# A short-convolution attention and a 16-expert layer on one core: the experts' narrow feature block first, and another order for the first tile

## The chip, the cores and the metric

The kernel runs on one core of a Trainium2 chip. The metric is the device time of one execution in microseconds (us). Names used below: TensorE (PE in the profile, with its weight loads as PEld), VectorE (DVE), ScalarE (ACT), GpSimd (POOL), and SP, the queue that issues most DMAs. Each engine works through its own instructions in program order and waits for others through semaphores; the order in the program is therefore the schedule.

## The reference, cut to what matters

All data is float32. `x` and the context are 8 batches of 256 rows of 512 features: 2048 rows (`T`), in 16 tiles of 128.

```python
# attention: k = v = context, q = layernorm(x), heads of 8 rows, 32 heads
kv  = einsum('bhil,bhjl->bijhl', k, v)          # products of rows of one head
out = causal_convolution(kv, ssm_kernel) + kv * D
out = einsum('bijhl,bhil->bjhl', out, q)
x   = x + out
# experts: 16 experts, the best 4 for each row, 256 slots each, inner width 352
h      = layernorm(x)
scores = softmax(h @ gate_w.T); topk_w, topk_i = top_k(scores, 4)    # weights normalised
xg     = tokens gathered for each expert                              # 16 x 256 x 512
mid    = silu(xg @ w_gate) * (xg @ w_up)                              # 512 -> 352
y      = scatter_add((mid @ w_down) * weight)                         # 352 -> 512
x      = x + y + (silu(h @ sw_gate) * (h @ sw_up)) @ sw_down          # shared part, width 704
```

## The kernel before

The schedule is written by hand: every engine gets its instructions in the order in which the program calls them.

**Attention.** A loop over 16 tiles of 128 rows, two heads each, in the order 1, 0, 2, 3, ... (tile 1 is `FIRST`, because its convolution matrices come straight from the input). `heads_of` transposes a tile on TensorE and copies it out of PSUM twice on ScalarE (L418, L419); `normalise` writes the normalised rows on ScalarE (L369 `nmr`, L370); `products` multiplies rows of k, one instruction for each of four chunks on GpSimd (L443, L445, and L451 for later heads). `attend` runs the convolutions as matmuls (L468) into one of two PSUM tiles `y`, and VectorE multiplies by q and sums (L501 to L518); the last sums are on GpSimd or VectorE (L520, L521). The PSUM pool `ps_tr` has two buffers under one tag for all transposes, logits and warm-up transposes (`stir`, L669). Ahead of the loop, tile 1's k is transposed, then its x is normalised, eight warm-up transposes run, and q is transposed. `begin` finishes a convolution matrix, `pads` and `windows` write the others to memory, from where they are loaded (`toep`); the shared weights (`swg`, `swu`, `swt`, `swd`) follow on SP, nine pieces for a tile.

**What fills TensorE.** `fill(n)` runs n steps of the shared part (L154, L168, L185) between the attention's steps. Every fourth tile `logits_of` computes the router's logits of four tiles (L592) and copies them to `exch` on ScalarE (L600); `turn_logits` transposes that (L612) and copies it to `logits` on VectorE (L615), and `choose` picks the experts of one tile at a time.

**Experts.** A loop over 16 experts. The weights of expert e + 2 are loaded at the end of iteration e into two buffers (`w`, `wd`). An expert's 352 inner features are blocks of 128, 128 and 96: `NI` is 3, `NW` is 2, the last block (index 2) is the narrow one. `gate_up` takes a wide block with 16 float32 matmuls (L1025; each is two instructions), a silu on ScalarE (L1032) and a product on VectorE (L1033). The narrow block uses weights packed side by side by `pack` on ScalarE into the one buffer `wt` (L1008): 8 matmuls of 64 columns for gate and up of the last 32 features (L1037) and 4 of 128 columns for the first 64 (L1045), then silu and product in three pieces (L1054, L1055, L1058, L1059). `down` multiplies the three blocks for each half of the 256 slots (L1067), scales (L1075) and adds the rows to `out` by an indirect DMA on GpSimd's queue (L1076); every such scatter waits for the one before to land. Between gate-up and down stand, for the experts ahead, `tokens` (L994, L404 on VectorE), `find` (L911 on TensorE, L919 to L934 on VectorE) and `gather` (L968, GpSimd). `find` and `gather` serve expert e + 3 and so end with expert 12; `shuffle` (`slots`, `gb`, on SP) follows the weights' load.

The last expert does its two halves one after the other, so that the first half's scatter runs under the second half's matmuls.

Of the kernel before, what the change touches and what calls it, by code (L numbers as in the profile page):

```python
# [20 lines left out]
P = 128  # L21
# [7 lines left out]
HT = R // HD  # L29
HB = HD * B  # L30
E, K, CAP, I, IS = 16, 4, 256, 352, 704
# [22 lines left out]
def ssm_attention__then__moe_kernel(  # L54
# [22 lines left out]
    nc = tc.nc  # L77
# [182 lines left out]
    with ExitStack() as att:  # L260
# [11 lines left out]
        FIRST = 1  # L272
# [140 lines left out]
        def heads_of(src, width, name):  # L413


            dst = half.tile([P, NC, HT, width], F32, name=name)
            pt = transpose_in(src).rearrange("p c (h w) -> p c h w", h=HT)
            nc.scalar.copy(dst[:, :, :, 0:HB], pt)  # L418
            nc.scalar.copy(dst[:, :, :, HB:width], pt[:, :, :, 0 : width - HB])  # L419
            return dst  # L420
# [14 lines left out]
            )  # L435
            return toep if head < PLAIN else toep.rearrange("p m q -> p (m q)")

        def products(head, hh, k2):

            kv = work.tile([P, NC + 1, PAIRS], F32, name="kv", bufs=3)  # L440
            kh = k2[:, :, hh, :]
            kc = kh.ap[1][0]
            nc.gpsimd.tensor_mul(kv[:, 0:NC, ND * HB :], kh[:, :, 0 : HB // 2], kh[:, :, HB // 2 : HB])  # L443
            for c in range(NC):
                nc.gpsimd.tensor_mul(  # L445
                    kv[:, c, 0 : ND * HB].rearrange("p (d w) -> p d w", d=ND),
                    kh[:, c, 0:HB].unsqueeze(1).broadcast_to([P, ND, HB]),
                    view(kh[:, c, :], 0, [[B, ND], [1, HB]]),
                )
            if head >= PLAIN:  # L450
                nc.gpsimd.tensor_add(kv[:, NC, :], kv[:, 0, :], kv[:, 1, :])  # L451
            return kv
# [229 lines left out]

        qn = load.tile([P, L], F32, name="qn", tag="kn")
        stats = first_statistics(xs[:, FIRST, :])
        k2 = heads_of(loaded.pop(FIRST), KW, "k2")
        normalise(qn, xs[:, FIRST, :], *stats)
        begin(0)
        kvs = [products(FIRST * HT, 0, k2)]
        stir(8)
        q2 = heads_of(qn, QW, "q2")  # L690
        toeps.update({FIRST * HT + hh: firsts[hh] for hh in range(HT)})
        stats = first_statistics(xs[:, 0, :])
# [31 lines left out]
        for n in range(NT):  # L724
            more = n + 1 < NT
            swift = n + 1 in SWIFT
            t = seq[n]
            oT = work.tile([P, NC, P], F32, name="oT")
            tps = [toeps.pop(t * HT + hh) for hh in range(HT)]
            if swift and more:  # L730
                got_k = fetch_blocks(sent_k)
            if more and n:
                for hh in range(HT):
                    load_blocks(seq[n + 1] * HT + hh)
            if swift and more:
                got_q = fetch_blocks(sent_q)
            for i in range(2 if n == 0 else n + 3, min(n + 4, NT)):
                loaded[i] = load_tile(i)
            load_shared(9)
            attend(t * HT + 0, 0, 0, tps[0], kvs[0], q2, oT)  # L740
            if n == 0:
                begin(1)
                kvs.append(products(t * HT + 1, 1, k2))
            if n - 2 in MILD:
                transpose_blocks(xnT[:, :, n - 2, :], got_x)
            choose()
            if more and not swift and n:
                qn = load.tile([P, L], F32, name="qn", tag="kn")
                stats = statistics(qn, xs[:, seq[n + 1], :])
            fill(2)  # L750
            if n + 2 in SWIFT:
                kp, kp_by_block = in_blocks("kp")
                kp_stats = statistics(kp_by_block, chunked(xs[:, n + 2, :]))

            attend(t * HT + 0, 0, 2, tps[0], kvs[0], q2, oT)
            if more and not swift:
                if n == 0:
                    qn = load.tile([P, L], F32, name="qn", tag="kn")
                k_next = heads_of(loaded.pop(seq[n + 1]), KW, "k2")
                normalise(qn, xs[:, seq[n + 1], :], *stats)  # L760
            if n > 0:
                total = add_to_x(seq[n - 1], oT_done)
            fill(2)
            if n > 0:
                xn, xstats = new_statistics(seq[n - 1], total)
            if more:
                if swift:
                    k_next = heads_from(got_k, KW, "k2")
                kv_next = [products(seq[n + 1] * HT, 0, k_next)]

            attend(t * HT + 1, 1, 0, tps[1], kvs[1], q2, oT)
            if more and not swift:
                q_next = heads_of(qn, QW, "q2")
            if n == 0:
                pg = ps_tr.tile([P, NC, P], F32, name="pg", tag="pt")
                for c in range(NC):
                    nc.tensor.transpose(pg[:, c, 0:E], every(gw, c), ident[:E, :E])
                nc.scalar.copy(gwT[:, :, 0:E], pg[:, :, 0:E])
            fill(2)
            if n > 0:  # L780
                if n - 1 not in MILD:
                    normalise(xn, xs[:, seq[n - 1], :], *xstats)
                store(seq[n - 1], xstats)
            if more:
                if swift:
                    q_next = heads_from(got_q, QW, "q2")
                kv_next.append(products(seq[n + 1] * HT + 1, 1, k_next))
            if n + 2 in SWIFT:
                nc.scalar.copy(kp_by_block, chunked(loaded.pop(n + 2)))
                sent_k = send_blocks(kp)  # L790
            if n - 2 in MILD:
                ready(n - 2)

            attend(t * HT + 1, 1, 2, tps[1], kvs[1], q2, oT)
            turn_logits()
            if n == 0:
                windows()
            if n - 1 in MILD:
                got_x = fetch_rows(n - 1)
            elif n > 0:  # L800
                turn(seq[n - 1], xn)
                fill(1)
                ready(n - 1)
            fill(1)
            if n + 2 in SWIFT:
                qp, by_block = in_blocks("qp")
                normalise(by_block, chunked(xs[:, n + 2, :]), *kp_stats)
                sent_q = send_blocks(qp)
            if n in (6, 7, 8):
                next(making)  # L810
            choose()
            oT_done = oT
            if more:
                kvs, q2 = kv_next, q_next
# [196 lines left out]
            )  # L1011
        return wt

    def gate_up(xgT, mid, w, wt, cols, fs=range(NI)):

# [44 lines left out]

    def down(e, n, mid, wd, wg):
        po = ps_ex.tile([P, L], F32, name="eo", tag="ex")
        for f in range(NI):
            m = min(P, I - f * P)
            nc.tensor.matmul(  # L1067
                po,
                lhsT=mid[:m, f, n * P : (n + 1) * P],
                rhs=wd[:m, f, :],  # L1070
                start=(f == 0),
                stop=(f == NI - 1),
            )
        o = ffn.tile([P, L], F32, name="eo_sb", bufs=3)
        nc.vector.tensor_scalar_mul(o, po, wg[:, n : n + 1])  # L1075
        nc.gpsimd.indirect_dma_start(  # L1076
            out=out,
            out_offset=bass.IndirectOffsetOnAxis(ap=idx[:, e, n : n + 1], axis=0),
            in_=o,
            in_offset=None,  # L1080
            compute_op=ALU.add,
        )
# [4 lines left out]
        moved[e] = shuffle(gathered[e])  # L1087
    fill(6)
    xgT_next = tokens(0)
    gathered[AHEAD - 1] = gather(AHEAD - 1)  # L1090
    moved[AHEAD - 1] = shuffle(gathered[AHEAD - 1])
    while behind:
        fill(1)
    for e in range(E):
        w, wd = experts.pop(e)
        wt = pack(w)
        xgT, wg = xgT_next
        mid = ffn.tile([P, NI, CAP], F32, name="mid")
        if e + 1 < E:
            gate_up(xgT, mid, w, wt, slice(0, CAP))  # L1100
            xgT_next = tokens(e + 1)
            if e + AHEAD < E:
                find(e + AHEAD, hots.pop(e + AHEAD))
                gathered[e + AHEAD] = gather(e + AHEAD)
            for n in range(NSL):
                down(e, n, mid, wd, wg)
            if e + AHEAD + 1 < E:
                hots[e + AHEAD + 1] = compare(e + AHEAD + 1)
        else:

            gate_up(xgT, mid, w, wt, slice(0, P))
            gate_up(xgT, mid, w, wt, slice(P, CAP), range(0, 1))
            down(e, 0, mid, wd, wg)
            gate_up(xgT, mid, w, wt, slice(P, CAP), range(1, NI))
            down(e, 1, mid, wd, wg)
        if e + 2 < E:
            experts[e + 2] = load_expert(e + 2)
        if e + AHEAD < E:
            moved[e + AHEAD] = shuffle(gathered[e + AHEAD])
# [38 lines left out]
```

## Time and profile before

| what | value |
|---|---|
| time before, median of 3 runs (range) | 691.94 us (690.48 to 692.03) |
| the profiled execution: time, span | 687.52 us, 685.8 us |
| TensorE busy / weight loads | 658.9 us (96%) / 486.3 us |
| VectorE, ScalarE, GpSimd busy | 386.9, 184.6, 323.6 us |
| mean granted TensorE clock | 0.995 |
| experts (first gate-up matmul to last down matmul) | 421.6 to 674.2 us, one expert about 15.7 us |
| last scatter issued, end | 677.5 us, 685.8 us |

Spans and starts are in us from the start of the span. A row of the timeline gives start, duration, engine, line, operation, what is written from what, and in brackets the idle time before it and what ended it. In the rows of groups, the number after `|` is the busy time in total, then the mean in ns of one, then the idle time ahead of them. Matmuls are pipelined and their bars overlap, so what a matmul costs is read from the distance between two starts. A float32 matmul of the program shows as two instructions.

### The profile page before, as it was taken

The numbers are of one execution on the slowest core, as the hardware profiler recorded it, in microseconds if no ns is written. First come the engines' busy times: TensorE is split into PE (matmuls) and PEld (weight loads), VectorE is DVE, ScalarE is ACT, GpSimd is POOL, SyncE is SP. The second block draws the span as 40 slices with busy tenths as digits, with TensorE's granted clock in tenths as the row PEclk, the third lists the DMA queues.
The fourth block names the chain that finished last, engine by engine and source line by source line (L and its number), as shares of the span: only waits on it lengthen the run. The fifth ranks groups of instructions, "written<-read, shape, count | busy, mean of one in ns | idle before, by whom it ended". The sixth has DMA issues, their size and how long they took to land. (4 is left out here: it accounts for less than half of the span.)

```text
span 685.8 us, 9781 instructions
## 1 busy us (share of the span) xinstructions
PE 658.9 (96%) x3313; PEld 486.3 (71%) x3313; DVE 386.9 (56%) x930; ACT 184.6 (27%) x465; POOL 323.6 (47%) x479
## 2 busy tenths in 40 slices
PE   7889999998999999999999999999999999999993
PEld 6677977777867877876868686776666777777662
DVE  3956676878867776676545621444555554443230
ACT  2464433444342343412322010111211111111110
POOL 5676546877675676546210310344434434333121
PEclk9999999999999999999999999999999999999997
DMA  6683455555556535441018461688899899999943
GB/s 136 231 250 97 130 162 131 149 135 159 136 141 182 139 99 152 115 112 46 16 47 284 118 195 37 200 254 251 251 268 264 256 264 283 262 269 259 267 82 44
DMA packets 98438, 117.79 MB, mean 172 GB/s; under 512 B 11267, under 2 KB 64355, under 8 KB 98388
## 3 DMA queue, kind: packets, MB, share of 16 engines
q1 hardware_dynamic: 90932, 99.86, 48.6%
q0 software_dynamic: 7168, 17.04, 12.5%
q10 hardware_dynamic: 288, 0.26, 0.3%
q8 instruction: 26, 0.43, 0.3%
q14 instruction: 24, 0.20, 0.1%
HBM read 84.25 MB, written 32.88 MB: 171 GB/s over the span
## 5 line engine op out<-in xcount | busy, mean ns | idle before, releaser
L468 PE MATMUL y<-kv,toep 128*128 128x288 f32 x528 | 139.3, 408 | 3.1 <-DVE f L518 2.8
L1076 POOL DMA_INDIRECT out<-eo_sb,idx x32 | 67.1, 2098 | 121.9 <-DMA wd<-in_L_ffn_w_down 35.8
L468 PEld LDWEIGHTS y<-kv,toep 128*128 128x128 f32 x528 | 99.5, 191 | 33.9 <-issue 7.8
L1025 PE MATMUL pgu<-xgT,w 128*128 128x256 f32 (+1 forms) x544 | 113.7, 367 | 0.0
L1025 PEld LDWEIGHTS pgu<-xgT,w 128*128 128x128 f32 x544 | 98.7, 190 | 19.9 <-issue 8.2
L1067 PE MATMUL eo<-wd,mid 128*128 128x512 f32 (+1 forms) x192 | 89.8, 606 | 0.9 <-DVE mid L1059 0.9
L520 POOL TENSOR_TENSOR f<-f 128x256 f32<-128x256 f32 x60 | 43.8, 729 | 91.4 <-DVE f L518 84.2
L445 POOL TENSOR_TENSOR kv<-k 128x256 f32<-128x256 f32 x128 | 85.8, 704 | 0.0
L968 POOL DMA_INDIRECT g<-xw_d,ido x32 | 33.8, 1056 | 98.7 <-DVE idx L934 59.2
L168 PE MATMUL sgu<-xnT,swg 128*128 128x256 f32 (+1 forms) x400 | 78.0, 338 | 0.0
L168 PE MATMUL sgu<-xnT,swu 128*128 128x256 f32 (+1 forms) x400 | 77.8, 337 | 0.0
L185 PE MATMUL so<-swd,smid 128*128 128x512 f32 x160 | 73.9, 593 | 0.0
L168 PEld LDWEIGHTS sgu<-xnT,swg 128*128 128x128 f32 x400 | 65.3, 191 | 7.3 <-issue 0.2
L168 PEld LDWEIGHTS sgu<-xnT,swu 128*128 128x128 f32 x400 | 64.6, 191 | 6.3
L1067 PEld LDWEIGHTS eo<-wd,mid 128*128 128x128 f32 (+1 forms) x192 | 34.0, 189 | 43.6 <-issue 23.8
L1032 ACT ACTIVATE eact<-pgu 128x256 f32<-128x256 f32 (+1 forms) x34 | 12.6, 372 | 166.0 <-PE pgu L1025 166.0
L1033 DVE TENSOR_TENSOR mid<-eact,pgu 128x256 f32<-128x256 f32 (+1 forms) x34 | 13.8, 405 | 71.1 <-ACT eact L1032 71.1
L491 DVE TENSOR_TENSOR y<-y,again 128x576 f32<-128x576 f32 x28 | 21.4, 766 | 57.2 <-PE y L468 37.2
L185 PEld LDWEIGHTS so<-swd,smid 128*128 128x128 f32 x160 | 29.9, 190 | 31.9 <-issue 30.4
L177 ACT ACTIVATE act<-sgu 128x256 f32<-128x256 f32 (+1 forms) x50 | 17.1, 341 | 122.6 <-PE sgu L168 122.6
L518 DVE TENSOR_TENSOR f<-y,z 128x512 f32<-128x512 f32 x64 | 44.3, 692 | 6.2
L517 DVE TENSOR_TENSOR y<-y,q 128x512 f32<-128x512 f32 x64 | 44.8, 699 | 2.2
(171 smaller groups left out, 806.2 us busy)
## 6 DMA issues: line engine op xcount, KB each, us to landing
w<-in_L_ffn_w_gate SPq DMA_DIRECT2D x16, 704.0 KB, 6.7
w<-in_L_ffn_w_up SPq DMA_DIRECT2D x16, 704.0 KB, 8.6
toep<-win_d SPq DMA_DIRECT2D x28, 320.0 KB, 5.2
wd<-in_L_ffn_w_down SPq DMA_DIRECT2D x16, 512.0 KB, 10.7
slots<-g SPq DMA_DIRECT2D x16, 512.0 KB, 4.1
gb<-slots SPq DMA_DIRECT2D x64, 128.0 KB, 4.1
got<-sent SPq DMA_DIRECT2D x26, 256.0 KB, 3.0
xs<-in_x SPq DMA_DIRECT2D x16, 256.0 KB, 6.6
```

The lines of the kernel that those rows point to most:

```text
L168: nc.tensor.matmul(pgu[:, k, :], lhsT=sw[:, c, f * P : (f + 1) * P], rhs=toks[:, c, :], start=(c == 0), stop=(c == NC - 1),)
L185: nc.tensor.matmul(po, lhsT=m[:, i * P : (i + 1) * P], rhs=swd[:, (f - 1) % (NF + 1), :], start=(f == 0), stop=(f == NF),)
L445: nc.gpsimd.tensor_mul(kv[:, c, 0 : ND * HB].rearrange("p (d w) -> p d w", d=ND), kh[:, c, 0:HB].unsqueeze(1).broadcast_to([P, ND, HB]), v ...
L468: nc.tensor.matmul(out, lhsT=toep[:, m * P : (m + 1) * P], rhs=rhs, start=(n == 0), stop=(n == len(pairs) - 1),)
L491: nc.vector.tensor_add(y[:, :, 0:PAIRS], y[:, :, 0:PAIRS], again.unsqueeze(1).broadcast_to([P, 2, PAIRS]),)
L517: nc.vector.tensor_mul(yd, yd, view(qq, 0, [[qc, 2], [B, ND], [1, HB]]))
L518: nc.vector.tensor_add(f, yd, z[:, :, :, BACK : BACK + HB])
L520: adder.tensor_add(f[:, :, 0:2, :], f[:, :, 0:2, :], f[:, :, 2:4, :])
L968: nc.gpsimd.indirect_dma_start(out=g[:, n, :], out_offset=None, in_=xw_d[:, :], in_offset=bass.IndirectOffsetOnAxis(ap=ido[:, e, n : n + 1 ...
L1025: nc.tensor.matmul(pgu[:, k, cols], lhsT=w[:, k, c, f * P : (f + 1) * P], rhs=xgT[:, c, cols], start=(c == 0), stop=(c == NC - 1),)
L1067: nc.tensor.matmul(po, lhsT=mid[:m, f, n * P : (n + 1) * P], rhs=wd[:m, f, :], start=(f == 0), stop=(f == NI - 1),)
L1076: nc.gpsimd.indirect_dma_start(out=out, out_offset=bass.IndirectOffsetOnAxis(ap=idx[:, e, n : n + 1], axis=0), in_=o, in_offset=None, comp ...
```

## The change

Four edits. In the experts, `gate_up` takes the narrow block first and `down` multiplies it first; the packing of expert e + 1's narrow weights is called right after `gate_up` of expert e instead of at the beginning of iteration e + 1, and that of expert 0 before the last gather. The last expert's second half does the narrow block between the first half's gate-up and its down. In the attention, `turn_logits` moves from right after the last `attend` of a tile to the end of the iteration, after `fill` and `choose`. For the first tile, x is normalised before k is transposed and copied, VectorE computes chunks 1 and 2 of the first head's products, and five warm-up transposes stand in the place of eight.

```diff
-        def products(head, hh, k2):
+        def products(head, hh, k2, helped=()):
...
             for c in range(NC):
-                nc.gpsimd.tensor_mul(
+                (nc.vector if c in helped else nc.gpsimd).tensor_mul(
...
         stats = first_statistics(xs[:, FIRST, :])
+        normalise(qn, xs[:, FIRST, :], *stats)
         k2 = heads_of(loaded.pop(FIRST), KW, "k2")
-        normalise(qn, xs[:, FIRST, :], *stats)
         begin(0)
-        kvs = [products(FIRST * HT, 0, k2)]
-        stir(8)
+        kvs = [products(FIRST * HT, 0, k2, helped=(1, 2))]
+        stir(5)
         q2 = heads_of(qn, QW, "q2")
...
             attend(t * HT + 1, 1, 2, tps[1], kvs[1], q2, oT)
-            turn_logits()
...
             choose()
+            turn_logits()
             oT_done = oT
...
-    def gate_up(xgT, mid, w, wt, cols, fs=range(NI)):
+    def gate_up(xgT, mid, w, wt, cols, fs=(I // P, *range(I // P))):
...
         po = ps_ex.tile([P, L], F32, name="eo", tag="ex")
-        for f in range(NI):
+        for k, f in enumerate((NW, *range(NW))):
             m = min(P, I - f * P)
             nc.tensor.matmul(
                 po,
                 lhsT=mid[:m, f, n * P : (n + 1) * P],
                 rhs=wd[:m, f, :],
-                start=(f == 0),
-                stop=(f == NI - 1),
+                start=(k == 0),
+                stop=(k == NW),
             )
...
     xgT_next = tokens(0)
+    wt_next = pack(experts[0][0])
     gathered[AHEAD - 1] = gather(AHEAD - 1)
...
-        wt = pack(w)
+        wt = wt_next
         xgT, wg = xgT_next
         mid = ffn.tile([P, NI, CAP], F32, name="mid")
         if e + 1 < E:
             gate_up(xgT, mid, w, wt, slice(0, CAP))
+            wt_next = pack(experts[e + 1][0])
             xgT_next = tokens(e + 1)
...
             gate_up(xgT, mid, w, wt, slice(0, P))
-            gate_up(xgT, mid, w, wt, slice(P, CAP), range(0, 1))
+            gate_up(xgT, mid, w, wt, slice(P, CAP), (NW,))
             down(e, 0, mid, wd, wg)
-            gate_up(xgT, mid, w, wt, slice(P, CAP), range(1, NI))
+            gate_up(xgT, mid, w, wt, slice(P, CAP), range(NW))
             down(e, 1, mid, wd, wg)
```

## Prediction

> **What bounds the kernel now.** I read the page first, then the waits of TensorE, its timeline in narrow windows, and last the queue of GpSimd and the chain that ended last.
>
> ```profile
> PE 658.9 (96%) x3313; PEld 486.3 (71%) x3313; DVE 386.9 (56%) x930; ACT 184.6 (27%) x465; POOL 323.6 (47%) x479
> L1067 PE MATMUL eo<-wd,mid 128*128 128x512 f32 (+1 forms) x192 | 89.8, 606 | 0.9 <-DVE mid L1059 0.9
> ```
> TensorE is busy 96% of the span. A gain must be a hole on TensorE, or something after its last matmul at 674.2. The second row owns to only 0.9 us of idle time before the down products, so the reorder of the experts looks worth 0.9 us. It is not the whole of it:
>
> ```profile
> 448.97 0.59 PE L1067 MATMUL eo<-wd,mid 128*128 128x512 f32 x1
> 449.52 0.70 PE L1067 MATMUL eo<-wd,mid 96*128 96x512 f32 x1
> 450.05 0.59 PE L1067 MATMUL eo<-wd,mid 96*128 96x512 f32 x1
> 638.23 0.70 PE L1067 MATMUL eo<-wd,mid 96*128 96x512 f32 x1 [0.45 <-DVE mid L1059]
> PEld eo L1067 <- DVE mid L1059: 13.2, 16, 1.3
> ```
> The first three rows are expert 1. Columns are start, duration, engine and line. Undisturbed down matmuls start 0.43 us apart (448.54 to 448.97). The step to 449.52, the first that needs the last 96 features, is 0.55, and the next 0.53: 0.12 + 0.10 = 0.22 us lost under overlapping bars. The fourth row is expert 13, which has no `find` between gate-up and down: 637.19 to 638.23 is 1.04, so 0.61 + 0.10 = 0.71 lost. The last row, from the waits, is the weight loader waiting for the same tile 16 times.
>
> Two holes in the attention, from the waits of TensorE:
>
> ```profile
> PE sgt L154 <- issue: 2.4, 1, 2.4
> PE lt L612 <- ACT exch L600: 1.7, 1, 1.7
> ```
> And the end, GpSimd's queue of scatters and the chain that ended last:
>
> ```profile
> 485.98 3.18 POOL L1076 DMA_INDIRECT out<-eo_sb,idx  x1 [0.30 <-issue]
> ...
> 644.94 1.56 POOL L1076 DMA_INDIRECT out<-eo_sb,idx  x1 [4.06 <-issue]
> 655.06 1.56 POOL L1076 DMA_INDIRECT out<-eo_sb,idx  x1 [8.56 <-DVE xgT L404]
> 660.75 1.56 POOL L1076 DMA_INDIRECT out<-eo_sb,idx  x1 [4.12 <-DVE mid L1033]
> 666.31 1.56 POOL L1076 DMA_INDIRECT out<-eo_sb,idx  x1 [4.00 <-DVE mid L1033]
> 671.90 1.56 POOL L1076 DMA_INDIRECT out<-eo_sb,idx  x1 [4.04 <-issue]
> 677.51 1.55 POOL L1076 DMA_INDIRECT out<-eo_sb,idx  x1 [4.05 <-issue]
> ```
> The last four start 5.6 us apart, each after the landing of the one before (median to landing 5.6). The last has its data at 674.21 + 0.75 = 674.96 and goes at 677.51, 2.55 us late. So the end belongs to the scatters: whatever TensorE saves reaches it only as far as the scatters move too. The 10.1 us from 644.94 to 655.06 cover expert 15's weight load, issued from 643.84 on.
>
> **First tile.** ScalarE now does `nmr` and `qn` before the two copies of k. By the rows of before: rstd ends at 7.89 on GpSimd, nmr 7.93, qn 8.27 to 9.08, the first copy from 8.99 (the next instruction came 0.72 after such a row at 36.87), the second 9.47 to 9.80, against 9.59 before. GpSimd's first product row thus slips 0.2, and its first chunk ends at 10.77 instead of 10.53. VectorE takes chunks 1 and 2. It has nothing else then, but the same shape (L520) took 0.42 us alone (33.15) and 1.00 beside GpSimd's products (19.99); I take the latter, done at 11.85, and fully one behind the other everything would be done at 12.3. The second chunk is due by the third convolution matmul, 11.76, the third chunk later: hidden; one behind the other, 0.4 of the gain goes. Behind the two products on VectorE wait tile 0's statistics and `pads` (0.69 + 0.18 + 0.15 + 0.71): from 11.85 that ends at 13.6 at the latest, when VectorE's first attention product is due at 13.4, so up to 0.2 may go; the `toep` loads that SP holds behind the pad are due at 20.67 and land near 17.4 now, so that slip is hidden.
>
> TensorE: eight stirs take 0.214 each from 8.54, five end at 9.61. q's transposes need k's PSUM buffer, so they wait for the copy at 9.80 and run to 10.77. The convolutions start at 10.8 instead of 11.59, 0.8 earlier. What that is worth depends on the clock:
>
> ```profile
> 11.59 0.69 PE L468 MATMUL y<-kv,toep 128*128 128x288 f32 x1
> 12.55 0.46 PE L468 MATMUL y<-kv,toep 128*128 128x288 f32 x1
> ```
> The first steps (11.59, 12.07, 12.55) are 0.48 us, the later ones 0.24, though the windows' granted clock says 1.00 all along: TensorE turns fast at about 12.65. If it does so at the same moment, six matmuls from 10.8 start at 10.80, 11.28, 11.76, 12.24, 12.66, 12.90; the sixth started at 13.33. I take 0.45 us; bounds 0 (products one behind the other, and slow clock for longer) and 0.8 (already fast, or slow in both).
>
> The Trainium skill ("TensorE: Matmul & The Clock Gate", Part 1) says the clock doubles only after a sustained busy window of about 3.4 us that runs freely, so starting earlier does not move the moment. The row agrees with a doubling; by that rule the start is worth the 0.45, and by a plain shift of rows 0.8. The skill ("SBUF — State Buffer", Who interferes with whom) also says that a VectorE instruction with two SBUF inputs fully blocks against GpSimd's reads, which is the 1.00 us row; by it the products run one behind the other and the start is worth less.
>
> This shift survives to the 2.4 us hole at 41.58: VectorE runs back to back from 13.85 to 24.04, GpSimd then from 24.12 to `less` at 31.24, which SP stores (31.27), so the blocks load at 33.03 and `swt` at 35.44, landing 6.0 later. All hangs on VectorE's first product, none on a fixed time. **−0.45.**
>
> **Logits' transpose, after the shared step.** Before, TensorE stood from 125.58 to 127.25 for ScalarE's copy of `exch`, queued behind q's and kp's copies. The copy does not move (127.2). The shared step of 0.9 us now fills the hole; 0.8 stays. The other three times nothing was waited for, and VectorE takes the logits later in its queue, ahead of choices that are not due until the routing: nothing. **−0.9** (bounds −0.3 if the shared step finds its PSUM bank taken, and −1.7).
>
> **Experts.** The 96 features' matmuls move to the front, so their three activations and three products run under 7.0 us of other matmuls. Down now ends on feature block 1, whose product is ready 0.95 us after gate-up (648.77 to 649.72 is that pair), while four down matmuls, 1.72, come first: no wait. Saved: 0.22 for each of experts 0 to 12, 0.71 for 13 and 14; 2.86 + 1.42 = 4.3 us of TensorE. The change of neighbour costs about 0.1 where the 64-column matmuls begin (444.03 to 444.34 instead of 0.22), before as after.
>
> Packing ahead moves nothing on ScalarE: between gate-up's last activation and the pack there was nothing to pass. It now must be ready at the next expert's first matmul. In expert 14 the pack ended at 654.26 and the next gate-up began at 657.50: 3.2 us of cover; without it, up to 0.9 an expert. Pack 0 goes ahead of shared blocks' activations (0.92 under gaps of 3.07 us): nothing. `w`'s last reader is now 3.1 us later, and SP's queue stands at that load with the down weights, slots and gb behind it. For expert 1 that load went at 448.87, gate-up ended at 447.19: still free. For expert 0 it slips from 428.75 to 431.5, before down weights that go at 437.53 anyway.
>
> VectorE reaches `find` 1.3 us earlier after gate-up (product at +0.95 instead of 449.46 − 447.19 = 2.27). GpSimd's gathers, which waited for it, go up to 1.3 earlier. This may help the scatters or only crowd them; I take zero, bounds −1.3 and +1.
>
> **What reaches the end.** From expert 3's first scatter (485.98) to expert 13's second (655.06) there are ten rounds and 10.12 us: (169.08 − 10.12) / 10 = 15.90 per expert, against TensorE's 15.73. Up to expert 3 the scatters follow TensorE, so they start 0.45 + 0.9 + 3 × 0.22 = 2.0 earlier. With a round of p the end moves by −2.0 − 10 × (15.90 − p). Experts 13 and 14 save nothing at the end, since the scatters after 655.06 are already one behind the other. If the round shortens with TensorE by about 0.2, p = 15.70: −4.0 us. On the profiled execution: 687.52 (span 685.8 and 1.7 around it) becomes 683.5. The median of the runs is 691.94, 4.4 above that execution; the same 4.0 off it gives 687.9.
>
> **Rivals.** (1) The chain stops binding: gathers come early, p = 15.5, −6 us, 685.9. For it: single rounds of 15.0 and 15.2 occur. (2) The DMA keeps its pace: p stays 15.90, −2.0, 689.9. For it: the DMA share is 0.91 to 1.00 in most experts from 563 on. (3) Slower: the same traffic in less time makes each scatter wait longer behind weight loads. Its place is the pair 644.94 to 655.06 and its like; rounds of 16.3, 16.8 and 17.8 occur. It decides from p = 16.1 (no change) and is slower by over 0.3% from p = 16.31; at 16.4 it costs 3.0, 694.9. (4) The packing does nothing of itself: by the rows above it only permits the order, which is already in the sum.
>
> **How the numbers follow.** Forecast 0.57, rival 1 0.15, rival 2 0.20, rival 3 0.08. 0.3% of 691.94, about what a measurement can tell from no change, is 2.08 us. Forecast and rival 1 are nearly all faster; rival 2 lies at the edge, a third of it faster. Faster 0.74, same 0.19, slower 0.07. The range runs from 685.4 (rival 1 with the start's full 0.8) to 691.0 (rival 2 without the start's gain and with little of the logits': 0.66 of experts 0 to 2 and 0.3).
>
> **What would show it.** Right: down's steps all 0.43; gate-up beginning with the 64-column matmuls with no wait for `wt`; expert period near 15.5; the wait for `lt` near 0.8; the first convolution near 10.8; the last scatter still some us behind its data. Wrong: a wait before L1037, the hole at 41.58 not moved, or scatter rounds at 15.9 or above.

## Result and profile after

| | before | after |
|---|---|---|
| median of 22 runs each, taken together (range) | 691.88 us (689.95 to 693.93) | 691.33 us (686.94 to 696.35) |
| ratio after / before, 95% interval | | 0.9994 [0.9973, 1.0014] |
| the profiled execution: time, span | 687.52, 685.8 us | 693.31, 691.6 us |
| down's matmuls, busy | 89.8 us | 86.4 us |
| last down matmul ends / last scatter is issued | 674.2 / 677.5 us | 676.7 / 683.1 us |

No change that the measurement can tell, where 4.0 us less were forecast. The profile of after is of an execution 2 us above its median and that of before of one 4.4 below, so their difference of 5.8 us is not the change's. First the page's row of the engines and the group of down:

```profile
PE 657.2 (95%) x3310; PEld 488.1 (71%) x3310; DVE 386.1 (56%) x932; ACT 185.1 (27%) x465; POOL 314.8 (46%) x477
L1067 PE MATMUL eo<-wd,mid 128*128 128x512 f32 (+1 forms) x192 | 86.4, 598 | 0.0
```

The repair inside the experts took place: the idle time before down is gone (0.0 where 0.9 stood), and the hidden 0.22 us of each expert with it, as TensorE's timeline shows:

```profile
433.70 5.40 PE L1067 MATMUL eo<-wd,mid 96*128 96x512 f32 x12
439.03 1.09 PE L1037 MATMUL pgu<-xgT,wt 128*64 128x128 f32 x16
...
596.03 1.09 PE L1037 MATMUL pgu<-xgT,wt 128*64 128x128 f32 x16 [1.95 <-ACT wt L1008]
627.85 1.09 PE L1037 MATMUL pgu<-xgT,wt 128*64 128x128 f32 x16 [0.76 <-ACT wt L1008]
645.08 1.09 PE L1037 MATMUL pgu<-xgT,wt 128*64 128x128 f32 x16 [2.15 <-ACT wt L1008]
```

Twelve instructions of down now run as one unbroken stretch from 433.70 to 439.03, 0.44 us apart. The last three rows are new: before experts 11, 13 and 14 TensorE stands still until ScalarE has packed `wt`. In TensorE's waits that is the longest entry of the whole span, 4.9 us against the 4.3 that the reorder was to save:

```profile
PE pgu L1037 <- ACT wt L1008: 4.9, 3, 2.1
PE sgt L154 <- issue: 3.2, 1, 3.2
PE lt L612 <- ACT exch L600: 0.8, 1, 0.8
```

The third row was 1.7 before; the second was 2.4. GpSimd's queue, expert 3's first scatter, expert 13's two and the last:

```profile
485.74 1.62 POOL L1076 DMA_INDIRECT out<-eo_sb,idx  x1 [0.30 <-issue]
...
650.60 1.56 POOL L1076 DMA_INDIRECT out<-eo_sb,idx  x1 [4.12 <-DVE mid L1059]
660.65 1.56 POOL L1076 DMA_INDIRECT out<-eo_sb,idx  x1 [8.49 <-issue]
...
683.14 1.55 POOL L1076 DMA_INDIRECT out<-eo_sb,idx  x1 [4.14 <-issue]
```

Expert 3's first scatter is 0.24 us earlier than before, not 2.0; expert 13's second is 5.6 later. Ten rounds with the same 10.05 us of the pair at 650.60 to 660.65 give (174.91 − 10.05) / 10 = 16.49 us per expert, against 15.90 in the profile before. From there to the end nothing changed (22.49 us, before 22.45).

**Why `wt` is late.** The next rows are SP's queue, the DMA issues of the stretch 630 to 646, and ScalarE, all for expert 14's weights.

```profile
625.72 0.38 SPq L980 DMA_DIRECT2D slots<-g  x1
631.26 1.88 SPq L983 DMA_DIRECT2D gb<-slots  x4
633.26 0.38 SPq L849 DMA_DIRECT2D w<-in_L_ffn_w_gate  x1
633.68 0.43 SPq L850 DMA_DIRECT2D w<-in_L_ffn_w_up  x1
```
```profile
w<-in_L_ffn_w_up SPq DMA_DIRECT2D x1, 704.0 KB, 10.4
```
```profile
644.11 0.92 ACT L1008 COPY wt<-w 128x512 f32<-128x512 f32 x2 [5.91 <-DMA w<-in_L_ffn_w_up]
```

Read them as a chain: `gb` waits 5.2 us on SP until `slots` has landed, the weights go directly behind it at 633.26, land 10.4 us after their issue, the pack runs 644.11 to 645.03, and the gate-up starts at 645.08. The buffer of `w` had been free since expert 12's gate-up, which ended near 620. The load therefore did not go late because its buffer or its data were late, but because of what stands before it in SP's queue. SP's waits in the experts of after:

```profile
SPq L983 <- DMA slots<-g: 73.4, 13, 8.3
SPq L980 <- DMA g<-xw_d,ido: 66.2, 13, 6.7
```

The first was 58.2 us in the profile before. The second closes the loop: `slots` waits for gathers, which GpSimd issues behind scatters, each waiting for the landing of the scatter before.

### The profile page after: what moved, and what is told of

Read it like the earlier page. It is cut to its first block, busy times and chain, and to the rows that moved or that the text cites. A ratio compares the mean times of both kernels' runs of the same rounds, so it can differ in the third digit from the quotient of the medians.

```text
span 691.6 us, 9761 instructions
## 1 busy us (share of the span) xinstructions
PE 657.2 (95%) x3310; PEld 488.1 (71%) x3310; DVE 386.1 (56%) x932; ACT 185.1 (27%) x465; POOL 314.8 (46%) x477
## 3 DMA queue, kind: packets, MB, share of 16 engines
q0 software_dynamic: 7168, 17.04, 12.5%
## 5 line engine op out<-in xcount | busy, mean ns | idle before, releaser
L468 PE MATMUL y<-kv,toep 128*128 128x288 f32 x528 | 140.9, 411 | 3.1 <-DVE f L518 2.7
L1076 POOL DMA_INDIRECT out<-eo_sb,idx x32 | 56.2, 1756 | 147.1 <-DMA wd<-in_L_ffn_w_down 73.6
L1067 PE MATMUL eo<-wd,mid 128*128 128x512 f32 (+1 forms) x192 | 86.4, 598 | 0.0
L520 POOL TENSOR_TENSOR f<-f 128x256 f32<-128x256 f32 x60 | 43.8, 729 | 92.7 <-DVE f L518 87.4
L968 POOL DMA_INDIRECT g<-xw_d,ido x32 | 36.7, 1146 | 85.4 <-DVE idx L934 43.8
L1075 DVE TENSOR_SCALAR eo_sb<-eo,wg 128x512 f32<-128x512 f32 x32 | 24.0, 749 | 34.8 <-PE eo L1067 23.6
```

Source lines behind the costliest of these rows:

```text
L468: nc.tensor.matmul(out, lhsT=toep[:, m * P : (m + 1) * P], rhs=rhs, start=(n == 0), stop=(n == len(pairs) - 1),)
L520: adder.tensor_add(f[:, :, 0:2, :], f[:, :, 0:2, :], f[:, :, 2:4, :])
L968: nc.gpsimd.indirect_dma_start(out=g[:, n, :], out_offset=None, in_=xw_d[:, :], in_offset=bass.IndirectOffsetOnAxis(ap=ido[:, e, n : n + 1 ...
L1067: nc.tensor.matmul(po, lhsT=mid[:m, f, n * P : (n + 1) * P], rhs=wd[:m, f, :], start=(k == 0), stop=(k == NW),)
L1076: nc.gpsimd.indirect_dma_start(out=out, out_offset=bass.IndirectOffsetOnAxis(ap=idx[:, e, n : n + 1], axis=0), in_=o, in_offset=None, comp ...
```

## Experiments

Each kernel is told with the edit, the expectation as it was written, and the result; ratios are to runs of the kernel before, taken beside it on the same chip. The round is the ten scatter rounds of one profiled execution, divided by ten as above.

**Each part alone.** The kernel before with one of the parts: the experts' part (`exp`), the first tile's (`first`), and the move of `turn_logits` (`logits`).

```diff
 exp, against after:
-        normalise(qn, xs[:, FIRST, :], *stats)
         k2 = heads_of(loaded.pop(FIRST), KW, "k2")
+        normalise(qn, xs[:, FIRST, :], *stats)
...
-        kvs = [products(FIRST * HT, 0, k2, helped=(1, 2))]
-        stir(5)
+        kvs = [products(FIRST * HT, 0, k2)]
+        stir(8)
...
+            turn_logits()
...
             choose()
-            turn_logits()
 first, against before: the first two edits above, the other way round
 logits, against before: the third edit above, the other way round
```

> Before, with the experts' part of the change alone (narrow block first, weights packed ahead, last expert's order). Theory A, the transfers pace the experts: TensorE's period falls to 15.5 us but the scatter rounds stay at 15.9 or above and waits for wt appear ahead of the 64-column matmuls; the time stays within 1 us of before. Theory B, a slow-clock stretch after the hole near 42 us eats the gain of the whole change: nothing near 42 us is touched here, so this kernel gains its 4 us, 0.994 of before.

> Before, with the first tile's part alone (x normalised first, VectorE's help, five warm-up transposes). Theory A: the start is 0.4 us earlier and that is all, 0.999 to 1.000 of before. Theory B: the earlier shared weights collide with other loads, the hole ahead of the first shared step grows past 3 us and the clock drops behind it in more executions: 1 to 2 us slower, with the granted clock at 0.5 for some us after 42.

> Before, with the logits' transpose moved alone. Both theories: the wait for lt falls from 1.7 to 0.8 us, everything after it comes 0.9 us earlier, 0.999 of before. Theory A adds that the last scatter moves by no more than that; if the time does not move at all, the experts' stage does not follow its own start.

| | median us (before 692.06) | ratio | round us, one profile | granted clock, that profile |
|---|---|---|---|---|
| `exp` | 690.42 | 0.9975 [0.9940, 1.0010] | 16.33 | 0.991 |
| `first` | 691.99 | 0.9984 [0.9948, 1.0019] | 16.39 | 0.984 |
| `logits` | 691.55 | 0.9984 [0.9951, 1.0017] | 16.22 | 0.993 |

No part alone can be told from no change. A gain of 4 us by the experts' part, 0.994, lies on the edge of its interval, so it is unlikely, but not excluded, that one part's gain is eaten by another. In `first`, half clock was granted after a hole of 2.90 us, much as its second theory had it, but no slower time is shown. In `logits` the wait for `lt` fell to 0.8. The experts' part brings the new wait by itself, as TensorE's waits of `exp` show:

```profile
PE pgu L1037 <- ACT wt L1008: 3.9, 3, 2.2
```

`first` and `logits` leave the experts as they were, and yet their rounds are 16.39 and 16.22, not 15.90. That made the 15.90 itself suspect.

**A second profile of both kernels,** unchanged.

> The kernel before once more, for a second profile. If its rounds of scatters (15.90 us in the profile shown) are typical, they are 15.9 again and the execution takes 687 to 688; if that execution was a lucky one, the rounds are 16.2 to 16.4, as in the two runs that leave the experts as they were.

> The changed kernel once more, for a second profile. Rounds of 16.3 to 16.6 again and waits for wt, by the theory that SP's order paces the experts; a first convolution near 11.0; the hole ahead of the first shared step between 1.4 and 3.3 us, by when its weights land.

Before took 690.95 us, after 692.17. GpSimd's queue of the second profile of before:

```profile
486.61 3.18 POOL L1076 DMA_INDIRECT out<-eo_sb,idx  x1 [0.30 <-issue]
...
659.45 1.56 POOL L1076 DMA_INDIRECT out<-eo_sb,idx  x1 [8.60 <-issue]
...
681.11 1.56 POOL L1076 DMA_INDIRECT out<-eo_sb,idx  x1 [4.02 <-issue]
```

Expert 13's first scatter goes at 649.29, so (659.45 − 486.61 − 10.16) / 10 = 16.27. The round of before is 15.90, 16.27, 16.39 and 16.22 in the four profiles with its expert code, 16.2 in the mean; with the new expert code it is 16.49, 16.33, 16.59 and 16.62 (of after, `exp`, `warm` below and after again), 16.5 in the mean. The highest of the first four is above the lowest of the others, so that the new order lengthens the round is likely, not shown. In the second pair, after is 3.7 us ahead at expert 3's first scatter (482.87 against 486.61) and 0.4 behind at expert 13's second (659.89 against 659.45): the ten rounds and the pair at their end (10.84 us, before 10.16) give back all of the lead. Not all of it is the change's: 2.2 us are there at the first shared step already (39.98 against 42.19), which waits for `swt` to land. The weights come late in before's expert code as well: ScalarE waits 17.3 us in 5 experts for `w` in the second profile of before, 22.9 in 6 in `first` and 16.6 in 6 in `logits`, and only in the first profile of before 0.4 in 1. But there TensorE does not need the packed copy until it has done both wide blocks (8 matmuls each, shown as 16 instructions), 7.0 us later, and its wait is not to be seen.

**Where the rounds are set: the data.** The down weights of experts 2 to 15 are not loaded, and those of experts 0 and 1 serve instead, in the kernel before and in after.

```diff
+    downs = []
...
     def load_expert(e):
...
+        if e >= 2:
+            return w, downs[e % 2]
         wd = wpool.tile([P, NI, L], F32, name="wd")
+        downs.append(wd)
```

> The kernel before, with the down weights of experts 2 to 15 not loaded (those of 0 and 1 are used again), which takes 0.70 MB of some 4.2 MB out of each expert's traffic. Theory A (transfers pace the experts, in rounds of 16.2 to 16.4 us where TensorE needs 15.73): the scatter rounds fall to TensorE's 15.73 and the end comes 3 to 6 us earlier than before. Theory C (the order of waits on SP's queue and the chain of scatters sets the rounds, not the amount of data): under 1.5 us earlier. If the clock alone made the differences: no change.

> The changed kernel with the same loads left out (the down weights of experts 0 and 1 used again). Theory A: no wait for wt is left, the scatter rounds follow TensorE at 15.5, and it is 3 to 5 us under the kernel before with the same loads left out, the gain that was forecast. Theory C: waits for wt stay, and it is within 1.5 us of that kernel.

685.29 us (ratio to before 0.9916 [0.9883, 0.9948]) without the change, and 681.08 (0.9845 [0.9802, 0.9887]) with it: 4.2 us apart, the size of the forecast; by the two intervals it is 4.9 ± 3.7. `lite_after` has no wait for `wt`, TensorE's expert period is 15.50, and the round of 15.28 is below it because expert 13's scatter no longer has gathers before it. The gain exists as soon as the scatters and loads leave room. The round of the kernel before stayed at 15.88, though 15.73 was expected; its end is earlier for the most part because the last pair of the ten rounds takes 5.52 us (647.64 to 653.16) in the place of some 10.1. But this edit removes data and also SP's waits for the `wd` buffer, so it cannot say which of the two mattered.

**The order of the queue, with the same data.** Expert e + 2's gate and up weights are issued on ScalarE's queue, right after expert e's gate-up, in after (`wq`) and in the kernel before (`wq_before`). The number of bytes is unchanged.

```diff
             gate_up(xgT, mid, w, wt, slice(0, CAP))
+            if e + 2 < E:
+                early_w[e + 2] = load_gate_up(e + 2, nc.scalar)
             wt_next = pack(experts[e + 1][0])
...
+    def load_gate_up(e, queue):
...
     def load_expert(e):
...
-        nc.sync.dma_start(out=w[:, 0], in_=w_gate[e].rearrange("(p c) f -> p c f", p=P))
-        nc.sync.dma_start(out=w[:, 1], in_=w_up[e].rearrange("(p c) f -> p c f", p=P))
+        w = early_w.pop(e) if e in early_w else load_gate_up(e, nc.sync)
```

> The changed kernel with the gate and up weights of expert e + 2 issued on ScalarE's queue right after gate-up of expert e, instead of on SP behind the blocks that wait for slots to land. Theory A (amount of data): the waits for wt go, but the scatters come no earlier, the time stays within 1 us of the changed kernel. Theory C (order): no wait for wt, rounds near 15.6, and 3 to 4 us under the changed kernel.

> The kernel before, with the gate and up weights of expert e + 2 issued on ScalarE's queue after gate-up of expert e, as in the run of the changed kernel with that edit (682.3 us). Theory: SP's order paces the experts in both orders, so this kernel gains too, but TensorE's period of 15.73 with its 4.3 us of holes is left: 686 to 687 us, 4 to 5 above that run. If the reorder of the experts is worth nothing even with the weights early: 682 to 683.

`wq` takes 682.32 us, 0.9864 [0.9821, 0.9907] of before; that is 9 us under after by the ratios, more than twice what theory C expected. Its ScalarE issues expert 14's weights at 617.87, 15.4 us earlier than in after, and never waits for `w`; here the same three instructions of another expert:

```profile
478.39 0.33 ACTq L849 DMA_DIRECT2D w<-in_L_ffn_w_gate  x1
478.77 0.45 ACTq L850 DMA_DIRECT2D w<-in_L_ffn_w_up  x1
479.31 0.93 ACT L1014 COPY wt<-w 128x512 f32<-128x512 f32 x2 [0.55 <-issue]
```

The two issues cost ScalarE 0.8 us, under gaps of several us. GpSimd's queue of `wq`:

```profile
487.58 1.62 POOL L1082 DMA_INDIRECT out<-eo_sb,idx  x1 [3.75 <-DVE mid L1061]
...
648.55 1.56 POOL L1082 DMA_INDIRECT out<-eo_sb,idx  x1 [3.95 <-issue]
...
671.08 1.55 POOL L1082 DMA_INDIRECT out<-eo_sb,idx  x1 [4.40 <-DVE eo_sb L1081]
```

The pair at the end has shrunk from 10.05 to 5.52 us (643.03 to 648.55), the round is (160.97 − 5.52) / 10 = 15.54, TensorE's own period of 15.50, and the last scatter goes 1.1 us after TensorE's last down matmul (670.0) instead of 6.5. Expert 13's second scatter is 12.1 us earlier than in after: 9.4 from the ten rounds and 4.5 from this pair, less 1.8, because expert 3's first scatter is later (487.58 against 485.74). From 430 to 660 the DMA engines are busy 0.93 of the time at 255 GB/s, in after 0.89 at 253: the amount of data was not the limit, the place of the issues was. SP's wait for `slots` is now 45.4 us in 11, and no weights for the gate-up stand behind it.

`wq_before` takes 685.01 us, 0.9927 [0.9904, 0.9949], with a round of 15.73, TensorE's period before the change. Against that, after with the same queue is lower by 0.0063 of 692, 4.4 us, each by the runs of before beside it; by the two intervals this is uncertain by some 3.4. Below, `wq_warm`, on the chip of `wq_before`, is 4.2 us under it. Both agree with the 4 to 5 us that were expected. So the reorder's gain is there once the weights go early. What this pair does not separate is an issue at an earlier time from an issue on another queue; it changes both.

**The scatter chain.** In after each of the experts' scatters goes to a memory of its own, so that none waits for the one before.

```diff
         nc.gpsimd.indirect_dma_start(
-            out=out,
+            out=apart[e * NSL + n],
...
+    apart = [out] + [
...
```

> The changed kernel with each scatter going to memory of its own, so that no scatter waits for the one before to land (the sum of the experts is thereby not formed). Same traffic. Theory A: the waits for wt stay; only the last links of the chain go, some 3 to 5 us off the end. Theory C: GpSimd's gathers go as soon as their index is there, slots and blocks and weights come earlier, the waits for wt vanish, and the end comes 6 us or more earlier.

680.81 us, 0.9852 [0.9812, 0.9891]. TensorE never waits for `wt`, and expert 14's weights go at 624.74 instead of 633.26. ScalarE still waits for `w`, 20.1 us in 9 experts, but 3.2 at the longest, where it was 6.2 in after. The weights stand on SP's queue as before; SP's wait for gathers has fallen from 66.2 to 20.4 us, that for `slots` has grown from 73.4 to 114.0. The group of the scatters in the page:

```profile
L1076 POOL DMA_INDIRECT apart<-eo_sb,idx x31 | 58.6, 1891 | 43.8 <-DVE eo_sb L1075 36.1
```

Their idle time is 43.8 us, mostly for their data; in after it is 147.1. So two links of the loop were cut separately, the weights' place on SP and the scatters' waits, and each cut ends TensorE's wait for `wt` and gives 9 to 10 us against before by its ratio.

**The hole before the first shared step.** TensorE stands before L154 for the load of `swt`. In after (`warm`) and in `wq` (`wq_warm`) 26 warm-up transposes fill it.

```diff
                 turn(seq[n - 1], xn)
+                if n == 1:
+                    stir(26)
                 fill(1)
```

> The whole change, with 26 more warm-up transposes on TensorE in the hole ahead of the first shared step (about 39 to 42 us), so that TensorE is never idle there. Theory B: the clock stays at full speed there, the slow executions vanish and the time is 3 to 4 us under before (0.995). Theory A: only the 1.7 us of a slow stretch, in those executions that had one, come back: about 1 us under the whole change, and the waits for wt and the late scatters stay.

> The changed kernel with the weights on ScalarE's queue and the 26 warm-up transposes in the hole near 42 us. If slow-clock stretches behind that hole still cost what they cost in the changed kernel (1.7 us in about half of the executions): 681.4, some 0.9 under the run without them. If they cost nothing at the end: 682.3.

`warm` is at 689.79 us, 0.9962 [0.9925, 0.9998]; the hole is gone (0.26 us left) and the clock stays full behind it, but after itself is within that interval, so a gain from it is not shown. `wq_warm` is at 680.77, 0.9857 [0.9823, 0.9891], by its ratio the same as `wq`, so its two expectations cannot be told apart. By their ratios both beat before, and after at 0.9994, by 9 to 10 us. What one such hole can do is seen in TensorE's timeline and windows (stretch, length, busy time of PE, PEld, DVE, ACT and POOL, granted clock, DMA share, GB/s) of after:

```profile
41.96 1.13 PE L154 MATMUL sgt<-xnT,swt 128*128 128x128 f32 x8 [3.22 <-issue]
42.93 3.01 PE L468 MATMUL y<-kv,toep 128*128 128x288 f32 x6
```
```profile
42.00:44.00 2.00, 2.00 (x11) 1.71 (x12) 0.29 (x1) 0.84 (x3) 2.00 (x4) 0.75 1.05 287
44.00:46.00 2.00, 2.00 (x7) 1.41 (x6) 0.02 (x1) 0.43 (x1) 1.92 (x4) 0.50 0.80 246
46.00:48.00 2.00, 2.00 (x18) 2.00 (x18) 1.86 (x5) 0.00 (x0) 0.13 (x1) 0.90 0.43 109
```

The same six convolution instructions took 1.62 us in the profile before and 3.01 here. From the granted clock, the half clock lasted 2 × (0.25 × 2) + 2 + 2 × (0.10 × 2) = 3.4 us, so it cost 1.7. It is not in every execution. In the second profile of before, with a hole of 2.83 us, the six instructions took 1.62 again, and in `wq`, with 3.02 us, too; `first` with 2.90 had it. A stretch of half clock also followed two waits for `wt`: 3.4 us after one of 2.48 us (after again, at 592.90) and after one of 4.33 (`warm`, at 645.97), so such a wait can cost 1.7 us more than itself. Among executions of one kernel the slower ones have the lower mean clock (after's with 0.993 and more took 686.9 to 693.2 us, those with 0.984 and less 692.6 to 696.4). The clock as recorded does not explain the missing gain: its mean over all executions is 0.989 in before (66 in the experiments) and in after (22).

## Why the prediction was wrong, step by step

**The bound was read rightly, its size was not.** "The end belongs to the scatters" held: the last scatter goes 6.5 us after TensorE's last down matmul, and the edits that moved the scatters moved the time (`wq`, `free_after`). The step that failed is **"What reaches the end"**, in its term p. It took 15.90 us for the round before from one execution that was 4.4 us under the median, and moved only the sum to the median. Four profiles put the round at 16.2. With that, TensorE's 15.73 was half a microsecond off the limit; "if the round shortens with TensorE by about 0.2", p = 15.70, had no row behind it, and after's four profiles have 16.5. What sets the round is the loop through SP's queue and the scatters that `wq` and `free_after` cut; with the weights early it is 15.54, near TensorE's period. With the mean rounds of the two codes, the prediction's own formula gives −2.0 + 10 × (16.5 − 16.2) = about +1 us, where −0.55 was measured with an interval of −1.9 to +1.0. (The lower end of the range is a slip as well: rival 1 with the start's full 0.8 adds up to 685.6, not 685.4.)

**The cover of the pack.** The prediction gave it 3.2 us from one expert, with "up to 0.9 an expert" without it. It priced the copy and not its input: ScalarE waited for `w` 31.5 us in 8 experts, and TensorE lost 1.95, 0.76 and 2.15 us. The narrow block needs the weights' landing and then 0.92 us of copy before the first matmul, where the wide block needs the landing alone. The one profile at hand, with its 0.4 us, showed none of this. The prediction did name what stands on SP's queue around the weights' load; it looked only at what waits behind it and at expert 0 and 1, not at what the load itself waits behind from expert 3 on.

**Experts, TensorE's side: held.** Down's steps are even, the holes of experts 13 and 14 are gone, and the expert's period, where no weights are late, is 15.50 us as named.

**First tile: held in the pair shown, by luck.** VectorE's two products took 1.40 us together, where 1.00 each had been taken; the convolutions start at 10.99 (10.8 named), and VectorE's first attention product is 0.41 earlier (0.45 named):

```profile
9.82 1.40 DVE L445 TENSOR_TENSOR kv<-k 128x256 f32<-128x256 f32 x2 [1.25 <-ACT k L419]
...
13.44 0.29 DVE L501 TENSOR_TENSOR z<-y,q 128x128 f32<-128x128 f32 x1 [1.12 <-PE y L468]
```

Over all profiles this does not hold. From the first transpose of k on TensorE to that product it takes 4.8 to 6.6 us in the six profiles with the old first tile (5.5 in the mean) and 5.2 to 6.8 in the eight with the new one (6.4 in the mean): later by 0.9, with overlapping ranges. "TensorE turns fast at about 12.65. If it does so at the same moment" was the weak point. In six of the eight new ones the convolutions begin at about 10.6 to 10.8 and still step 0.48 us after 12.5, until 13.2 to 15.2; in four of the six old ones they step 0.24 from 11.5 at the latest. The windows of `first` (columns as above) show the half clock that the prediction's bound 0 had as "slow clock for longer":

```profile
10.00:14.00 4.00, 3.42 (x7) 2.52 (x8) 1.90 (x6) 0.75 (x2) 3.57 (x9) 0.50 0.09 20
```

That the five warm-up transposes in the place of eight are the reason is likely, but no run changes them alone. "This shift survives to the 2.4 us hole at 41.58", with "none on a fixed time", failed too: in after `swt` is issued 0.51 us earlier (34.93 against 35.44), but it took 6.9 us to land instead of 6.0, and L154 starts at 41.96, later than before. Starts between 39.98 (after again) and 42.83 (`lite_after`) occur, so 0.4 us of shift is less than this load's spread.

**Logits: the wait held, the gain did not.** The wait for `lt` is 0.8, as named. But a new wait follows, in after and in `logits`, which before has not:

```profile
PE sgu L168 <- DVE tail L162: 0.4, 1, 0.4
```

The shared step that now comes first leaves its PSUM tile to VectorE's `tail`, which stands behind the attention's products in VectorE's queue, and two groups later TensorE waits for that tile. From the first logits matmul to the next time's it is 81.40 us in before, 81.18 in `logits` and 81.17 in after. So 0.2 of the 0.9 was won, a little less than the prediction's bound of 0.3 for a PSUM bank that is taken.

**How 2.0 became 0.24 at expert 3.** In the profiled pair the first shared step starts 0.38 later, the slow clock behind it costs 1.7, the logits give 0.24 and experts 0 to 2 give 0.66: TensorE should reach expert 3's down 1.2 later, and it does so 1.14 later (480.19 against 479.05). The scatter is nevertheless 0.24 earlier, because GpSimd's gathers ahead of it go 2.96 us after the down has begun instead of 4.33. That is the effect of up to 1.3 which the prediction named ("VectorE reaches `find` 1.3 us earlier") and took as zero.

**The rivals.** Rival 3 was right in the rounds (16.49, where it asked for 16.31) and in its resource, the weight loads; not in the time, since the typical before had long rounds too, and not in its place, since the pair it named takes 10.05 us against 10.12 before. Its mechanism was only half of it: not only scatters wait for weights, the weights wait for scatters too, through `gb`, `slots` and the gathers. Rival 2 (the round keeps its pace) was the nearest in kind, and at 689.9 the nearest in time, with 1.4 us still missing.

## What to carry to other kernels

Before a saving on the busiest engine is added up, look at what paces the loop, and take that pace from several executions: a round that differs by 0.3 us between two profiles outweighs a saving of 0.2 in each of ten. The same goes for a start that hangs on the clock: one pair of profiles showed the gain that had been forecast, fourteen profiles together showed none. When a step is moved to where its input is needed sooner, follow the input back through its transfer, the queue that issues it, and what that queue waits for at that place. A load whose buffer is free but which stands behind a waiting one is cheap to move: here the two issues took 0.8 us of ScalarE for each expert, and the time fell by more than twice the change's forecast.

## What the runs showed of the hardware

An idle time of 2 us and more on TensorE can be followed by 3.4 us at half the granted clock, or not. Ahead of the first shared step: yes after 3.22, 2.90 and 2.74 us (after, `first`, `lite_after`), no after 2.83, 3.02, 2.81 and 2.87 (before again, `wq`, `logits`, `wq_before`). Elsewhere: yes after 1.99 (`lite_before`, at 34.10), 2.48 (after again) and 4.33 (`warm`), no after 2.00 in the place of `lite_before`'s (`logits`, `wq_before`) and 2.15 (after, at 645.08). The Trainium skill ("TensorE: Matmul & The Clock Gate", Part 1) has the clock fall after an idle window of about 3.4 us and rise after a busy one of the same length, with windows that run freely. The length of the slow stretch agrees. That holes shorter than the stated window were enough differs from its table, and that the same hole sometimes costs nothing fits its remark on the phase.

Two products of 128x256 on VectorE took 1.40 us beside GpSimd's products of the same tile, where one alone takes 0.42 and one beside GpSimd 1.00 in the profile before. So one row of such a neighbourhood is no price for the next. Both engines were done with the first head's products at 11.78; one behind the other had been estimated at 12.3.
